# Keys and values by seven products ahead of the up projection, and up results masked and turned on chip

## The chip, the cores and the metric

One core of a Trainium2 chip runs the whole kernel in one launch. The metric is the device time of one execution in microseconds (us), the median of several runs. In rows of the profile, PE is TensorE's matmul, PEld its weight load, DVE VectorE, ACT ScalarE, POOL GpSimd, SP the SyncE queue that issues most DMAs.

## The reference

A post-norm decoder layer over x of 16 x 112 tokens of 1024 numbers (1792 tokens, 14 tiles of 128) with a context of 16 x 375 tokens (6000) of 1024:

```python
s = silu(x @ w_gate.T)                     # 1792 x 2752
s = s with the 1376 smallest |s| of each row set to 0
h = s * (x @ w_up.T)
x = layernorm(x + h @ w_down.T)
q, k, v = x @ Wq, ctx @ Wk, ctx @ Wv       # k, v: 256 wide, 8 heads of 32, each for 4 of 32 query heads
x = layernorm(x + softmax(q k.T / sqrt(32)) v @ Wo)
x = layernorm(x + x @ dequantized 4-bit weights, in bfloat16)
```

All products but the last are float32.

## The kernel before, in words

The work is one program for one core. Each engine's instructions are kept in the order in which they were written (`AsWritten`), so the order of the Python calls is the order of each engine's queue. Up to the down projection everything happens in `gates_up_keys`.

There a `stream` of work items is made: 24 plain gate chunks (`gate_chunk`, tiles 0 to 3, 464 or 456 columns), then 20 gate units and 28 up units (`up_unit`), then 16 x 5 items of keys and values (`kv_unit`). `emit` takes the next item, issues its matmuls into one of six PSUM banks (`ps_g`), and then issues the evacuation of the item before it (`behind`, `settle(1)`). Each item has a weight, about the columns of its eight-matmul product.

A gate or up unit takes two token tiles (a pair) and one of four column passes of each half of the 2752 columns (344 of 1376), and forms the four 128 x 344 results by seven products instead of eight (Strassen's method in Winograd's form; the order of the products is `ORDER`). A product is 4 f32 matmuls, 8 records in the trace. It needs sums of x tiles (`xs_d`, made once by `sums_of_x` on GpSimd) and sums of weight blocks (`sum_weights`, 16 instructions on GpSimd for each set of weights; a set serves 2 or 3 pairs of gates, or 7 pairs of up). The results are combined in the evacuations: in the gates by copies on ScalarE and adds on VectorE, two of which (L410, L417) read two SBUF tiles; in the up units those two run on GpSimd. Gate results go through silu to `s_d` in DRAM. Up results are multiplied with s (read back from `s_d`) on GpSimd (L393) and stored to `u_d`.

Beside the stream runs the search for the median of |s| of each row. `search(t)` handles one tile of 128 rows in 12 steps: the absolute values on ScalarE, seven counts (ScalarE counts 1824 columns at L556, VectorE 928 at L559), a selection (L622), the eight largest (L624), the mask (L638), and a flag over all rows (L641) on which VectorE branches: if a row was not settled, a slow search runs. Then the mask of 2752 bfloat16 goes to `m_d` by a DMA of the GpSimd queue (L647). Two searches alternate, and after each step `beside` emits `share` of the stream's weight. The share spreads the 14 searches over the stream up to its last 14 batches of keys and values:

```python
steps = len(DAMPS) + 6
ends = (B - 2) * (2 + NKP)
share = sum(w for w, _ in list(stream)[:-ends]) / (steps * TT)
```

`load_row(t)` first emits the stream until the gates of tile t are stored whole, and then loads the row tile from `s_d`. Rows of a pair become whole with the last pass of their weights.

Keys and values are computed per batch of 375 context tokens: two items of keys (256 outputs on the partitions, 375 columns, L452), three of values (tokens on the partitions, 256 columns, L460), each of 8 f32 matmuls. Beside them `next_turn` reads u and the mask back, multiplies them on GpSimd (L506), transposes the product on TensorE (L524, 308 transposes in all), copies it (L526) and stores it to `hT_d`, from which the down projection (`Down`, L827) loads its blocks. `load_down` loads down weights, `down.first_product` begins the down projection. Loads and most stores are issued on SP; `store_later` holds a store back by two items.

After that come the down projection's passes, queries, attention, the output projection and the 4-bit product; the change touches only how attention reads keys and values from `k_d` and `v_d`.

Of the kernel before, what the change touches and what calls it, by code (L numbers as in the profile page):

```python
# [22 lines left out]
P = 128  # L23
# [23 lines left out]
H_CHUNKS = [(h * FH + o, w) for h in range(2) for o, w in ((0, 512), (512, 512), (1024, 352))]  # L47
UPASS = 4
UW = FH // UPASS
# [85 lines left out]
def gates_up_keys(  # L135
    nc, tc, order, ident, xT, wg, wu, ctxT, wk, wv, s_d, m_d, u_d, xs_d, hT_d, k_d, v_d, down,
# [22 lines left out]
    search_ctx, io_ctx, w_ctx = (ExitStack() for _ in range(3))  # L159
# [5 lines left out]
    wpool = w_ctx.enter_context(tc.tile_pool(name="g_w", bufs=1, side="right"))  # L165

# [34 lines left out]
    def load_others():  # L201

        for tag, size, ts_ in (("lo0", 5120, (4, 5, 6, 7, 12)), ("lo1", 5632, (8, 9, 10, 11, 13))):
            o = room(lo, tag, f"xo_{tag}", size, len(ts_), KC, P)
            for i, t in enumerate(ts_):
                xts[t] = o[:, i]
                load_x(t)

    def sums_of_x(j):
# [14 lines left out]
        0: lambda: load_x(1), 4: lambda: load_pair(1), 6: load_others, 8: lambda: sums_of_x(2), 10: lambda: sums_of_x(3),  # L224
        11: lambda: sums_of_x(4), 12: lambda: sums_of_x(5), 13: lambda: sums_of_x(6),
        14: lambda: load_weights(0), 15: lambda: sums_of_x(0), 18: lambda: deque(sum_weights(0, 0), 0),
        20: lambda: sums_of_x(1), 21: lambda: load_first(0),
# [37 lines left out]
    sets = [(wg, p, js) for js in GATE_PAIRS for p in range(UPASS)]  # L265
    sets += [(wu, p, tuple(range(pairs))) for p in range(UPASS)]
    units = [(k, j) for k, (_, _, js) in enumerate(sets) for j in js]
    n_gate = sum(w is wg for w, _, js in sets for _ in js)
# [4 lines left out]
    def load_weights(k):  # L273

        w, p, _ = sets[k]
        if k % 2:
            u = room(upool[0], "w0", f"u0_{k}", 3 * KH * UW, 3, KH, UW)
            v = room(upool[0], "w1", f"u1_{k}", 4 * KH * UW, 4, KH, UW)
        else:
            u = room(lo, "lo0", f"u0_{k}", 5120, 3, KH, UW)  # L280
            v = room(lo, "lo1", f"u1_{k}", 5632, 4, KH, UW)
        for to, i, h in ((u[:, 0], 0, 0), (u[:, 2], 0, 1), (v[:, 0], 1, 0), (v[:, 1], 1, 1)):
            nc.sync.dma_start(to, w[:, ts(i, KH), ds(h * FH + p * UW, UW)])
        wts[k] = u, v
# [19 lines left out]
    def load_rest(i):  # L304

        j = units[i][1]
        a = rest[i] = room(upool[0], "l", f"xl_{i}", 3 * KH * P, 3, KH * P, bufs=2)
        nc.sync.dma_start(a[:, :2], xs_d[j].rearrange("p h k n -> p h (k n)")[:, 2:])
        nc.sync.dma_start(a[:, 2], xT[2 * j + 1][:, KH:].rearrange("p k n -> p (k n)"))

    def side_loads(i):
        if i + 1 < n_up:
            load_first(i + 1)
            load_rest(i + 1)
        if i == n_up - 4:
            load_keys()

    sums = deque()

    def side_weights(i, b):  # L320

        k, j = units[i]
        at, n = sets[k][2].index(j), len(sets[k][2])
        if at == b == 0:
            sums.append(sum_weights(k, 1))
        if b == 1 and at == 0 and k + 1 < len(sets):
            load_weights(k + 1)
        if b == 0 and at == n - 1 and k + 1 < len(sets):
            sums.append(sum_weights(k + 1, 0))
        for _ in range(1 if at else 2):  # L330
            while sums and next(sums[0], sums) is sums:
                sums.popleft()
# [4 lines left out]
    def load_s():  # L337
        if s_order:
            i, t, h = s_order.pop(0)
            k, j = units[i]  # L340
            s = room(io, "s", f"us_{i}_{t}_{h}", 512, UW, bufs=5)
            nc.sync.dma_start(s, s_d[2 * j + t][:, ds(h * FH + sets[k][1] * UW, UW)])
            s_ahead.append((i, t, h, s))

    def silu():

        while unsaid and unsaid[0][0] >= len(stream) + 2:
            _, i, t, h, a = unsaid.popleft()
            k, j = units[i]
            nc.scalar.activation(a, a, AF.Silu)  # L350
            last = sets[k][1] == UPASS - 1 and (t, h) == (1, 1)
            store_later(
                s_d[2 * j + t][:, ds(h * FH + sets[k][1] * UW, UW)], a,
                (2 * j, 2 * j + 1) if last else (),
            )

    def up_unit(i, what):

        k, j = units[i]
        p, gate = sets[k][1], i < n_gate  # L360
        adds = nc.vector if gate else nc.gpsimd
# [8 lines left out]
        if what == "A11 B11":  # L370
            if i == n_gate:
                for _ in range(4):
                    load_s()
            side_loads(i)
        m = ps_g.tile([P, 512], F32, tag="pg", name=f"pu_{i}_{what[:2]}_{b}")[:, :UW]
        for n in range(KH):
            nc.tensor.matmul(  # L377
                m, a[i][:, b, ts(n, P)], w[:, n, :], start=(n == 0), stop=(n == KH - 1)
            )
        side_weights(i, ORDER.index(what))  # L380

        def own(tag):
            st[tag] = room(upool[0], tag, f"{tag}_{i}", 384, UW, bufs=3 if tag == "u" else 2)
            return st[tag]

        def store(t, h, tag):
# [4 lines left out]
            *of, s = s_ahead.popleft()  # L391
            assert of == [i, t, h]
            nc.gpsimd.tensor_tensor(a, a, s, ALU.mult)  # L393
            store_later(u_d[2 * j + t][:, ds(h * FH + p * UW, UW)], a)
            load_s()

        def evacuate():
            silu()
            if what == "A11 B11":
                nc.scalar.copy(own("c11"), m)  # L400
            elif what == "S2 T2":
                nc.vector.tensor_add(own("u"), st["c11"], m)  # L402
            elif what == "A12 B21":
                nc.vector.tensor_add(st["c11"], st["c11"], m)
                store(0, 0, "c11")
            elif what == "S1 T1":
                nc.scalar.copy(own("m5"), m)
            elif what == "S4 B22":
                nc.vector.tensor_add(own("c12"), st["u"], m)
                adds.tensor_tensor(st["c12"], st["c12"], st["m5"], ALU.add)  # L410
                store(0, 1, "c12")
            elif what == "S3 T3":
                nc.vector.tensor_add(st["u"], st["u"], m)
            else:
                nc.vector.tensor_add(own("c21"), st["u"], m)
                store(1, 0, "c21")
                adds.tensor_tensor(st["u"], st["u"], st.pop("m5"), ALU.add)  # L417
                store(1, 1, "u")
# [3 lines left out]
    ctxs, kv = {}, {}  # L422

    def load_ctx(b):
        tag, size = ("w0", 3 * KH * UW) if b % 2 else ("ctx", KC * SK)
        ctxs[b] = room(upool[0], tag, f"ctx_{b}", size, KC, SK)
        nc.sync.dma_start(ctxs[b], ctxT[b])

    def load_keys():
        kv["k"] = upool[0].tile([P, KC, KVD], F32, tag="wk", name="wk_sb")  # L430
        nc.sync.dma_start(kv["k"], wk)
        load_ctx(0)

    def kv_unit(b, u):
        if b == u == 0:
            kv["v"] = room(upool[0], "w1", "wv_sb", 4 * KH * UW, KC, KVD)
            nc.sync.dma_start(kv["v"], wv)
            for tag, n in (("lo0", 10), ("lo1", 11)):
                to_load.extend(down.place(lo, tag, n, 1))
        next_turn()  # L440
        if u == 0 and b < B // 2:
            next_turn()
        if u == (1 if b else 0) and b + 1 < B:
            load_ctx(b + 1)
        if u in (1, 3):
            load_down()
        c = ctxs[b]
        pk = ps_g.tile([P, 512], F32, tag="pg", name=f"pk_{b}_{u}")
        if u < 2:
            n, w, to = P, SK, k_d[b, :, u, :]  # L450
            for kc in range(KC):
                nc.tensor.matmul(  # L452
                    pk[:, :SK], kv["k"][:, kc, ts(u, P)], c[:, kc, :],
                    start=(kc == 0), stop=(kc == KC - 1),
                )
        else:
            at = (u - 2) * P
            n, w, to = min(P, SK - at), KVD, v_d[b, ds(at, P), :]
            for kc in range(KC):
                nc.tensor.matmul(  # L460
                    pk[:n, :KVD], c[:, kc, ds(at, n)], kv["v"][:, kc, :],
                    start=(kc == 0), stop=(kc == KC - 1),
                )

        def evacuate():
            o = room(upool[0], "u", f"kv_{b}_{u}", 384, SK, bufs=3)
            if n < P:
                nc.gpsimd.memset(o[P - Q :, :w], 0.0)
            nc.scalar.copy(o[:n, :w], pk[:n, :w])
            store_later(to, o[:, :w])  # L470

        return evacuate
# [7 lines left out]

    to_turn = deque((t, c) for t in range(TT) for c in range(len(H_CHUNKS)))
    found, asked, ready = set(), deque(), deque()
    n_asked = 0

    def load_turn():

        nonlocal n_asked
# [1118 lines left out]
```

## Time and profile before

| | us |
|---|---|
| median of 3 runs | 2512.85 (2509.98 to 2514.65) |
| profiled execution, time | 2511.96 |
| profiled execution, span | 2510.2 |
| PE busy in the span | 2469.8 |
| stage: plain gates | to 157 |
| stage: gate units | 157 to 482 |
| stage: up units | 482 to 938 |
| stage: keys, values and turns | 938 to 1302 |
| first pass of down and after | from 1302 |

The stage bounds are where the first matmul of the next stage starts in the timeline, rounded. The granted TensorE clock is 0.992 of full speed over the span. The page is read as follows: its second part cuts the span into 40 slices of 62.8 us and gives the busy tenths of each engine in each; the groups give the mean time of one instruction and the idle time before it; the waits say who waited for whom. Durations of matmul records overlap in the groups (a 344-column record has a mean of 452 ns, but eight of them take 2.31 us in the chain), so the chain is the better place for the price of one. In a timeline row the columns are start, duration, engine, line, operation, tiles, count, and in brackets the idle time before it with what ended it.

### The profile page before, as it was taken

The numbers are of one execution on the slowest core, as the hardware profiler recorded it, in microseconds if no ns is written. First come the engines' busy times: TensorE is split into PE (matmuls) and PEld (weight loads), VectorE is DVE, ScalarE is ACT, GpSimd is POOL, SyncE is SP. The second block draws the span as 40 slices with busy tenths as digits, with TensorE's granted clock in tenths as the row PEclk, the third lists the DMA queues.
The fourth block names the chain that finished last, engine by engine and source line by source line (L and its number), as shares of the span: only waits on it lengthen the run. The fifth ranks groups of instructions, "written<-read, shape, count | busy, mean of one in ns | idle before, by whom it ended". The sixth has DMA issues, their size and how long they took to land.

```text
span 2510.2 us, 33282 instructions
## 1 busy us (share of the span) xinstructions
PE 2469.8 (98%) x10674; PEld 1555.1 (62%) x10674; DVE 1232.8 (49%) x2020; ACT 791.8 (32%) x1872; POOL 1139.6 (45%) x1145
## 2 busy tenths in 40 slices
PE   9999999999999999999999999999999999999998
PEld 4456666666666667777764444444666666767764
DVE  0257767655555552000000442157667877777764
ACT  0233333333323322222110000000455655555653
POOL 1755413336364633222200000023578788888874
PEclk9999999999999999999999999999999999999999
DMA  9567866877787759887764222266876778777774
GB/s 358 210 221 267 284 239 233 282 253 271 234 285 235 231 200 323 280 278 253 244 218 158 81 90 95 82 217 209 195 189 188 198 192 209 193 198 197 188 179 118
DMA packets 321749, 538.15 MB, mean 214 GB/s; under 512 B 41984, under 2 KB 238976, under 8 KB 317440
## 3 DMA queue, kind: packets, MB, share of 16 engines
q1 hardware_dynamic: 283136, 447.41, 56.3%
q0 software_dynamic: 23168, 61.66, 8.3%
q10 hardware_dynamic: 15232, 26.62, 3.4%
q8 instruction: 87, 1.43, 0.2%
q14 instruction: 126, 1.03, 0.1%
HBM read 331.37 MB, written 103.50 MB: 173 GB/s over the span
## 4 chain that ended last, share of the span: by engine, by line
PE 76%; DVE 2%; DMA 2%; ACT 2%; issue 1%; POOL 1%; SPq 1%; ACTq 0%; POOLq 0%; DVEq 0%
PE m L827 18%; PE pu_S L377 13%; PE pu_A L377 9%; PE pk L460 7%; PE bank L1218 7%; PE pk L452 6%; PE bank L1056 5%; PE sc L1126 4%; PE po L1181 3%; PE bank L1275 2%; PE pt L524 1%; ACT probs L1134 1%; DMA weights<-squares 1%; DVE nmax L1132 1%; DVE squares L1154 1%
## 5 line engine op out<-in xcount | busy, mean ns | idle before, releaser
L1143 POOL TENSOR_TENSOR probs<-probs,sums 128x1500 f32<-128x1500 f32 x128 | 344.2, 2691 | 122.6 <-DVE sums L1142 110.3
L1134 ACT ACTIVATE probs<-sc,nmax 128x375 f32<-128x375 f32 x512 | 286.9, 573 | 231.6 <-DVE nmax L1132 216.9
L1132 DVE TENSOR_REDUCE nmax<-sc 128x2 f32<-128x750 f32 x256 | 228.5, 932 | 136.6 <-PE sc L1126 136.6
L556 ACT ACTIVATE ja<-a,to 128x1824 int8<-128x1824 f32 x98 | 177.9, 1815 | 283.4 <-DVE to L616 268.6
L827 PE MATMUL m<-wd,h 128*128 128x512 f32 (+1 forms) x616 | 265.0, 592 | 0.0
L377 PE MATMUL pu_A<-u,xe 128*128 128x344 f32 x768 | 237.9, 453 | 1.9 <-DVE u L402 1.9
L377 PE MATMUL pu_S<-u,xe 128*128 128x344 f32 x768 | 237.8, 452 | 0.1
L1154 DVE STREAM_TRANSPOSE squares<-probs 128x1536 f32<-128x1536 f32 x128 | 224.1, 1751 | 17.5 <-DMA weights<-squares 10.6
L377 PE MATMUL pu_S<-u,xl 128*128 128x344 f32 x768 | 229.9, 452 | 0.0
L901 DVE TENSOR_TENSOR c<-u,m 128x512 f32<-128x512 f32 x7 | 4.8, 688 | 436.1 <-DMA h<-hT_d 354.9
L1056 PE MATMUL bank<-x1T,wq_sb 128*128 128x224 f32 x1008 | 210.6, 363 | 0.0
L1056 PEld LDWEIGHTS bank<-x1T,wq_sb 128*128 128x128 f32 x1008 | 188.3, 192 | 34.8 <-issue 31.2
L827 PEld LDWEIGHTS m<-wd,h 128*128 128x128 f32 (+1 forms) x616 | 116.8, 190 | 146.7 <-issue 145.4
L377 PEld LDWEIGHTS pu_A<-u,xe 128*128 128x128 f32 x768 | 145.8, 190 | 78.9 <-DVE u L402 3.0
L1218 PE MATMUL bank<-wo_sb,aT 128*128 128x256 f32 x832 | 194.2, 387 | 0.0
L377 PEld LDWEIGHTS pu_S<-u,xe 128*128 128x128 f32 x768 | 145.8, 190 | 76.6 <-issue 0.6
L377 PEld LDWEIGHTS pu_S<-u,xl 128*128 128x128 f32 x768 | 145.9, 190 | 76.2
L1218 PEld LDWEIGHTS bank<-wo_sb,aT 128*128 128x128 f32 x832 | 154.9, 191 | 46.1 <-issue 23.7
L1168 POOL DMA_DIRECT2D weights<-squares x320 | 178.6, 564 | 8.8 <-issue 4.1
L506 POOL TENSOR_TENSOR hs<-hs,hm 128x512 f32<-128x512 f32 (+1 forms) x84 | 90.0, 1078 | 199.6 <-DMA hm<-m_d 188.3
L460 PE MATMUL pk<-wv_sb,ctx 128*128 128x256 f32 (+1 forms) x768 | 173.3, 379 | 0.0
L452 PE MATMUL pk<-ctx,wk_sb 128*128 128x375 f32 x512 | 167.1, 478 | 0.0
(165 smaller groups left out, 3355.5 us busy)
## 6 DMA issues: line engine op xcount, KB each, us to landing
weights<-squares SPq DMA_DIRECT2D x704, 96.0 KB, 3.3
h<-hT_d SPq DMA_DIRECT2D x56, 640.0 KB, 4.5
weights<-squares POOLq DMA_DIRECT2D x320, 96.0 KB, 3.5
xe<-in_xT_dram SPq DMA_DIRECT2D x48, 512.0 KB, 5.1
xe<-xs_d SPq DMA_DIRECT2D x48, 512.0 KB, 5.9
xl<-xs_d SPq DMA_DIRECT2D x48, 512.0 KB, 5.0
ctx<-in_ctxT_dram SPq DMA_DIRECT2D x16, 1500.0 KB, 8.2
u<-in_wg_dram SPq DMA_DIRECT2D x32, 688.0 KB, 9.0
```

The costliest lines, as they stand in the source:

```text
L377: nc.tensor.matmul(m, a[i][:, b, ts(n, P)], w[:, n, :], start=(n == 0), stop=(n == KH - 1))
L452: nc.tensor.matmul(pk[:, :SK], kv["k"][:, kc, ts(u, P)], c[:, kc, :], start=(kc == 0), stop=(kc == KC - 1),)
L460: nc.tensor.matmul(pk[:n, :KVD], c[:, kc, ds(at, n)], kv["v"][:, kc, :], start=(kc == 0), stop=(kc == KC - 1),)
L556: nc.scalar.activation(ja, a[:, NV:], AF.Sign, bias=to, scale=-1.0, accum_out=st["sgn"])
L827: self.nc.tensor.matmul(bank, a[:r, k, :], b(k)[:r], start=(k == 0), stop=(k == HK - 1),)
L1056: nc.tensor.matmul(pq[:, :GT], self.wq_sb[:, kc, ts(mc, P)], self.x1T[g][:, kc, :], start=(kc == 0), stop=(kc == KC - 1),)
L1132: nc.vector.tensor_reduce(nmax[h], sc[h][:, :, :SK], AX.X, ALU.max, negate=True)
L1134: nc.scalar.activation(pr[:, i, :SK], sc[i // 2][:, i % 2, :SK], AF.Exp, bias=nmax[i // 2][:, i % 2 : i % 2 + 1], accum_out=sums[:, i : i ...
L1143: nc.gpsimd.tensor_tensor(pr, pr, sums.unsqueeze(2).to_broadcast([P, 4, SK]), ALU.mult)
L1154: nc.vector.transpose(sq[:, :, n % 2].rearrange("p k (i f) -> p k i f", f=Q), probs[:, n % 3].rearrange("p i (k f) -> p k i f", f=Q),)
L1168: queue.dma_start(wt[ts(m, Q), :, j], by_part[ts(j, Q), :, m])
L1218: nc.tensor.matmul(pp[:, :256], aT[:, h, r, :], wo_sb[:, h * REP + r, ts(i, 256)], start=(h == 0 and r == 0), stop=(h == 1 and r == REP - 1),)
```

## The change

The order of the stream becomes gates, keys and values, up.

- Keys and values are formed with the seven products too: six pairs of blocks of 500 context tokens (free columns), the contraction of 1024 in two halves, the 256 outputs in two halves. Both keys and values have outputs on the partitions now. The weight sums are made once (`sum_kv_weights`), the sums of context blocks on GpSimd (`sum_ctx`, 16 instructions of 128 x 500 for a pair). Values are then transposed on TensorE (`turn_values`) and copied on ScalarE. All the combining adds run on VectorE.
- The up passes are 384, 384, 384 and 224 columns wide. For each up result the mask is loaded with s; VectorE multiplies s with the mask (`mask_s`), GpSimd the result with that, TensorE transposes it three items later (`turn`), and it goes to `hT_d`. `u_d` and its traffic are gone. The two adds that ran on GpSimd in the up units run on VectorE.
- The searches get a fixed pace of 2400 units of stream weight per tile (`PACE`), so that the masks are there before the up units. The stream may be emitted beside them up to the last pair of keys and values.
- The SBUF pools change hands between stages (`gate_swap`, `kv_swap`, `up_swap`); the down weights are loaded during the up units. `k_d` and `v_d` are laid out over all 6000 context tokens.

The core of the diff:

```diff
+GATE_PASSES = [(0, 344), (344, 344), (688, 344), (1032, 344)]
+UP_PASSES = [(0, 384), (384, 384), (768, 384), (1152, 224)]
+KVN = 500
+KV_PAIRS = B * SK // KVN // 2
+PACE = 2400
...
     def load_s():
...
+            m = pools["w"].tile([P, UW], BF16, tag="um", name=f"um_{i}_{t}_{h}", bufs=5)[:, :n]
+            nc.sync.dma_start(s, s_d[2 * j + t][:, at])
+            nc.sync.dma_start(m, m_d[2 * j + t][:, at])
+    def mask_s():
+        if s_ahead:
+            *_, s, m = s_ahead[0]
+            nc.vector.tensor_mul(s, s, m)
...
+    def combine(st, what, m, own, done):
...
+        elif what == "S4 B22":
+            nc.vector.tensor_add(own("c12"), st["u"], m)
+            nc.vector.tensor_add(st["c12"], st["c12"], st["m5"])
+            done(0, 1, "c12")
...
+            nc.vector.tensor_add(own("c21"), st["u"], m)
+            done(1, 0, "c21")
+            nc.vector.tensor_add(st["u"], st["u"], st.pop("m5"))
+            done(1, 1, "u")
...
             nc.gpsimd.tensor_tensor(a, a, s, ALU.mult)
-            store_later(u_d[2 * j + t][:, ds(h * FH + p * UW, UW)], a)
+            to_turn.append((len(stream), i, t, h, a))
+            mask_s()
             load_s()
...
+    def sum_ctx(i, names):
...
+            for n in range(KH):
+                nc.gpsimd.tensor_tensor(
+                    out[:, n], ctxs[i, y][:, n], ctxs[i, z][:, n], ALU.subtract
+                )
+                yield
+    FIRST_SUMS = (("T1", "B12", "B11"), ("T2", "B22", "T1"))
...
+    def beside_kv(i, b, x):
+        if x == "k":
+            if b == 0:
+                if i == 0:
+                    sums.append(sum_ctx(i, FIRST_SUMS))
+                    sum_some(8)
+                sums.append(sum_ctx(i, (("T3", "B22", "B12"),)))
+            if b == 2:
+                sums.append(sum_ctx(i, (("T4", "B21", "T2"),)))
...
+                if b == 5:
+                    sums.append(sum_ctx(i + 1, FIRST_SUMS))
...
+        sum_some(2)
+    def kv_unit(i, b, x):
...
+        turns_of_values()
...
+        m = products(
+            f"p{x}_{i}_{what[:2]}", what, lambda n: kv[x][:, o, n, :], ctxs[i, name]
+        )
+        beside_kv(i, b, x)
...
+    def turns_of_values(behind_=2):
+        while values_to_turn and values_to_turn[0][0] >= len(stream) + behind_:
+            _, at, c, a = values_to_turn.popleft()
+            turn_values(at, c, a)
...
+    def kv_swap():
+        settle(0)
+        silu(-NT)
+        issue(-NT)
+        w_ctx.close()
+        pools["kv"] = w_ctx.enter_context(tc.tile_pool(name="u_kv", bufs=1, side="right"))
+        load_ctx(0, 1, 1)
+        load_ctx(0, 1, 0)
...
+    for i in range(KV_PAIRS):
+        for b in range(len(ORDER)):
+            for x in "kv":
+                stream.append((KVN / 2, lambda i=i, b=b, x=x: kv_unit(i, b, x)))
+    stream.append((0, up_swap))
+    for i in range(n_gate, n_up):
+        for what in ORDER:
+            stream.append((sets[units[i][0]][2] / 2, lambda i=i, what=what: up_unit(i, what)))
...
-    ends = (B - 2) * (2 + NKP)
-    share = sum(w for w, _ in list(stream)[:-ends]) / (steps * TT)
+    ends = (n_up - n_gate) * len(ORDER) + 1 + 2 * len(ORDER)
+    share = PACE / steps
```

## The prediction

> **What bounds the kernel now.** I read the page first, then TensorE's waits, the chain, the windows by stage, and the timelines of VectorE and GpSimd in the gate stage. The page:
>
> ```profile
> PE 2469.8 (98%) x10674; PEld 1555.1 (62%) x10674; DVE 1232.8 (49%) x2020; ACT 791.8 (32%) x1872; POOL 1139.6 (45%) x1145
> ...
> DVE  0257767655555552000000442157667877777764
> ...
> POOL 1755413336364633222200000023578788888874
> ```
>
> TensorE (PE) works 2469.8 of 2510.2 us. The DVE row shows its reserve: 5 to 7 tenths busy in the gate and up products (slices 2 to 14), none in the keys and values (slices 15 to 20). TensorE's own waits confirm the bound: before attention they are a few us.
>
> ```profile
> PE pt L524 <- POOL hs L506: 2.1, 1, 2.1
> PE pu_A L377 <- DVE u L402: 1.9, 2, 1.3
> ```
>
> The chain gives the price of one matmul record without the overlap that the group rows hold (an f32 matmul is two records):
>
> ```profile
> 394.60 6.94 PE pu_S L377 x24
> ...
> 1286.35 5.06 PE pk L452 x16
> 1291.74 10.36 PE pk L460 x48
> 1302.10 443.94 PE m L827 x1034
> ```
>
> So 0.289 us at 344 columns, 0.316 at 375, 0.216 at 256, 0.429 at 512. The windows give the engines by stage (up to 482 gates, to 938 up, to 1302 keys and values; columns: PE, PEld, DVE, ACT, POOL, clock, DMA):
>
> ```profile
> 157.00:482.00 325.00, 323.02 (x1115) 211.30 (x1114) 223.92 (x397) 127.29 (x201) 129.08 (x139) 1.00 0.75 261
> 482.00:938.00 456.00, 456.00 (x1577) 299.36 (x1576) 238.10 (x514) 136.27 (x172) 213.69 (x221) 1.00 0.74 250
> ```
>
> In the gates VectorE is 69% busy at one search in 65 us (the flags' reductions, L641, lie at 302.46 and 367.46). The change halves that distance, so I looked at what stops VectorE there. VectorE, then GpSimd:
>
> ```profile
> 302.46 0.27 DVE L641 TENSOR_REDUCE flag<-row 1x1 int32<-1x128 f32 x1
> 307.94 0.51 DVE L415 TENSOR_TENSOR c<-u,pu_A 128x344 f32<-128x344 f32 x1 [5.22 <-issue]
> 308.49 10.71 DVE L417 TENSOR_TENSOR u<-u,m 128x344 f32<-128x344 f32 x1
> ```
> ```profile
> 304.29 0.56 POOL L647 DMA_DIRECT2D m_d<-m  x1 [18.26 <-DVEq L121]
> 304.88 3.52 POOL L294 TENSOR_TENSOR u<-u 128x344 f32<-128x344 f32 x4
> 308.36 6.99 POOL L294 TENSOR_TENSOR u<-u,u 128x344 f32<-128x344 f32 x8
> 315.31 3.52 POOL L294 TENSOR_TENSOR u<-u 128x344 f32<-128x344 f32 x4
> ```
>
> The branch after the flag keeps VectorE 5.2 us. The mask's store sits in GpSimd's queue behind that branch, and the weight sums pile up behind it; once released they run back to back, and VectorE's add of two SBUF tiles (0.52 us elsewhere) does not finish before the last of them, 10.2 us late. After each of the first five mask stores one two-input VectorE instruction waited so: 6.0, 10.1, 10.2, 9.8 and 4.6 us, mean 8.2. TensorE felt little of it: out of service from 302.7 to 321.2 but for one add, VectorE cost TensorE 1.3 us. Six PSUM banks cover some 13 us, once.
>
> **The change part by part.**
>
> *Keys and values by seven products.* Before: 16 batches of 32 records at 0.316 and 48 at 0.216, 16 x 20.5 = 328 us. After: 6 pairs x 2 x 7 products x 8 records = 672 records of 500 columns, 0.429 x 500/512 = 0.419 us, 282 us. Minus 46 us, on the path.
>
> *Values turned on TensorE.* 24 results x 4 transposes = 96. Four lie between 951.18 and 951.62 in TensorE's timeline, 0.11 us each: plus 11 us. The 308 transposes of h keep their number.
>
> *Up products 384 wide and 224 once.* 1176 records at 0.289 x 384/344 = 0.323 and 392 at 0.196 (nearest row: the queries' 224 columns, 32 in 6.27 us) make 457 us, against 1568 x 0.289 = 453: plus 3 us.
>
> *The way of u through DRAM.* It takes away 84+28 stores and 84 loads, 39 MB, and its 4 us of waiting at the start of the keys (the two waits above, roughly). Its DMA time lies beside TensorE, which works all 456 us of the up window at DMA 0.74: the transfers themselves are worth nothing. The mask's product goes to VectorE, idle in the new up stage: 112 x 0.6 us more, plus 56 adds, is 100 us in 457. GpSimd keeps 112 products of 0.95 us. The turns come three products (8 us) behind, over a sum and a product of 2 us: hidden. VectorE waits at the swap some 5 us (loads land in 4.5), which the banks cover. I take 0 for these, 0 to 5 for the range.
>
> So TensorE's own work falls by 46 + 4 - 11 - 3 = 36 us.
>
> *The searches, one per 2400 units of stream.* A unit is 16.2 us / 1204 = 13.45 ns: 32.3 us per search. Before: (5040 + 20 x 1204 + 28 x 1204 + 3326)/14 = 4726 units, 64 us. Work of one search on VectorE, from starts in the timeline: six counts 2.10 each, first count 1.4, b 3.3, best 4.0, m 1.65, flag and branch 5.4: 28.4 us. It fits alone, but not with the adds of the products, 3.5 us per gate unit.
>
> Where do the dense parts lie? The loop asks for row 4 after 36 steps of 200 units (7200; 5040 are plain chunks, so near unit 1.8) and must first emit gates up to unit 7.7, where rows 4 to 7 are whole. From there 48 steps, 4 searches, run over 9600 units = 8 gate units to 15.7; then row 8 forces emission to 18.6. The last 7 searches take 16,800 units, 1700 in the gates and 15,100 in the keys, 4.3 pairs of six.
>
> Gates 7.7 to 15.7: TensorE 8 x 16.2 = 130 us. VectorE 4 x 28.4 + 8 x 3.5 = 142, plus the wait after each mask store: row 8.2 us, four times, 33. Less 13 us of cover: plus 32 us. Bounds for that wait: below, 0.4 us (the two-input L616 at 213.46, beside running sums, waited 0.36); above, 10 us. So 0 to 39.
>
> *Swap to the keys.* T2 needs a block of ctx loaded into the space of the gate weights, behind the last unit's stores on SP: about 2.5 us to the last silu, 5 landing, four GpSimd sums of 1.28 (row of 128x512, L220): 12.6 us, against two products of 3.35. Plus 6; 0 if the load comes early, 13 if nothing is covered.
>
> *Keys and values, 4.3 pairs beside 6.3 searches.* TensorE 4.3 x (47 + 2) = 211 us. VectorE 6.3 x 28.4 + 4.3 x 14 adds of 0.6 = 215, plus a wait after each mask store: GpSimd now has 16 ctx sums a pair, about 11 per mask, of 1.28 us. I keep 8.2 us as measured (0.4 to 14): 52. The cover is smaller: the turn of a value stands in TensorE's queue two products, 6.7 us, behind the product whose sum it reads, and all matmuls queue behind it. Plus 215 + 52 - 211 - 7 = 49 us; 0 to 85.
>
> Sum: -36 + 32 + 6 + 49 = +51 us on the profiled execution's 2512.0 us (span 2510.2 and 1.8 around it; the median is 2512.9, so no correction): 2563 us.
>
> [...]
>
> **The rivals.**
>
> *VectorE keeps up: faster.* If the pile behind a mask store lets VectorE in after one sum, as at 213.46, the stalls are 12 - 13, so none, in the gates, none in the keys, and 6 at the swap: 2512 - 36 + 6 = 2482. For it: sums that came as their data landed did let VectorE in. Against: none of the first five mask stores went so. It decides at a wait of 3.3 us per store: with a wait of x the stalls are 4x - 1 and 6.3x - 3, and they eat the 30 us left at 3.3.
>
> *Worse: lag feeds on itself.* A late VectorE delays the mask store, so GpSimd's sums (T2, weights) come late too and TensorE waits for them directly; the flag waits for a row DMA in an SP queue held by late stores. With the upper ends: -36 + 39 + 13 + 85 = +101, 2613. For it: GpSimd already waited up to 51 us at that store. Against: forced emission leaves VectorE pauses to catch up.
>
> *It doesn't do what it says.* Searches still running when up begins would move, not vanish; the count above ends them 1.7 pairs ahead, so I give it little, within the cases above.
>
> **How the numbers follow.** VectorE-bound dense parts 0.56; faster rival 0.24; nearly even, a wait near 3.3 us, 0.05; worse 0.15. Some 0.2% (5 us) is what a measurement of this kernel can tell from no change. Range 2484 to 2613: the low end reaches to the faster rival, the high one to the upper bounds. Faster 0.24, same 0.05, slower 0.71.
>
> **What would show it.** Right: TensorE's waits on DVE, on POOL's sums and before the value turns at 30 us or more in gates and keys together; VectorE 8 or 9 tenths busy there and slack in up; two-input adds of 5 to 14 us behind mask stores; TensorE records of keys and values at 0.42 us. Wrong: TensorE without waits up to the up stage (then 2482), or waits placed in the up stage or at its end.

## The result and the profile after

The change makes the kernel slower: 2579.98 us median (2578.94 to 2582.74) beside 2513.6 us for the kernel before, a ratio of 1.0268, 95% interval 1.0251 to 1.0286. The profiled execution has a span of 2577.1 us, 66.9 more than before. The page after, first part and four rows of the second:

```profile
PE 2454.0 (95%) x10148; PEld 1458.7 (57%) x10162; DVE 1376.0 (53%) x2274; ACT 792.6 (31%) x1892; POOL 1119.5 (43%) x1094
...
PE   9989987989889999999999999999989999999997
...
DVE  0374476568773233333331342238677777777764
...
POOL 1754312352434224242320000023487888888874
PEclk9999998999999999999999999999989999999999
```

TensorE has less work (2454.0 against 2469.8 us) in a longer span. The holes in its row (slices of 64.4 us, counted from 0) lie in slices 2, 5, 6, 8, 10 and 11, that is between 129 and 773 us, in the gates and the keys and values. The seven largest of TensorE's thirteen kinds of wait from 150 to 900 us (line, whom it waited for: us in total, times, longest):

```profile
PE pu_A L402 <- ACT m L417: 18.0, 3, 9.3
PE pv L644 <- DVE v_ops L425: 14.6, 4, 6.8
PE pu_S L402 <- DVE c L425: 11.6, 1, 11.6
PE pk_S L402 <- POOL T L562: 8.9, 1, 8.9
PE pv L644 <- DVE to L738: 4.7, 2, 2.4
PE pt L491 <- DMA u<-in_wu_dram: 4.2, 1, 4.2
PE pv L644 <- DVE off L743: 4.1, 2, 2.3
```

Before, this list held two entries of 2 us. Four of these seven releasers are VectorE, and the largest is a ScalarE copy; why that one is VectorE's doing too is seen below. The stages in windows (gates, keys and values, up; columns as in the prediction):

```profile
158.00:530.00 372.00, 335.96 (x1121) 216.68 (x1120) 217.44 (x434) 132.47 (x206) 121.55 (x137) 0.94 0.68 232
530.00:869.00 339.00, 304.64 (x764) 141.28 (x763) 220.00 (x420) 123.08 (x172) 144.08 (x119) 0.95 0.47 153
869.00:1365.00 496.00, 488.90 (x1876) 327.33 (x1875) 167.21 (x307) 71.66 (x192) 158.93 (x158) 1.00 0.72 232
```

The gates' 1121 records take 372 us (before: 1115 in 325), and the granted clock, 1.00 there before, is 0.94. The lines do not show a full VectorE: 58% busy in the gates, 65% in the keys. One stop in the gates shows what they hide. First all engines, then TensorE's own timeline, then two windows (the seventh column is the clock):

```profile
348.01 0.48 ACT L393 ACTIVATE u<-u 128x344 f32<-128x344 f32 x1
...
348.18 0.27 DVE L775 TENSOR_REDUCE flag<-row 1x1 int32<-1x128 f32 x1
348.38 0.49 DVE L414 TENSOR_TENSOR c<-c,pu_A 128x344 f32<-128x344 f32 x1
...
350.00 0.56 POOL L781 DMA_DIRECT2D m_d<-m  x1 [34.61 <-DVEq L125]
350.58 0.92 POOL L305 TENSOR_TENSOR u<-u 128x344 f32<-128x344 f32 x1
351.45 6.98 POOL L305 TENSOR_TENSOR u<-u,u 128x344 f32<-128x344 f32 x8
...
355.72 0.21 DVE L743 TENSOR_SCALAR off<-sgn,nlt 128x1 f32<-128x1 f32 x1 [6.85 <-issue]
...
356.52 5.39 DVE L750 SCALAR_TENSOR_TENSOR to<-off,to 128x1 f32<-128x1 f32 x1
...
362.01 1.81 ACT L690 ACTIVATE ja<-a,to 128x1824 int8<-128x1824 f32 x1 [13.52 <-DVE to L750]
...
363.82 0.42 ACT L417 COPY m<-pu_S 128x344 f32<-128x344 f32 x1
```
```profile
353.28 2.59 PE L402 MATMUL pu_S<-u,xe 128*128 128x344 f32 x8
364.30 4.96 PE L402 MATMUL pu_A<-u,xe 128*128 128x344 f32 x8 [8.43 <-ACT m L417]
```
```profile
364.00:370.00 6.00, 5.70 (x10) 3.54 (x11) 5.61 (x16) 5.24 (x7) 0.00 (x0) 0.50 0.28 67
374.00:384.00 10.00, 10.00 (x36) 6.55 (x35) 9.60 (x17) 3.48 (x7) 0.00 (x0) 1.00 0.80 303
```

The branch after the flag keeps VectorE 6.85 us. The mask's store, queued behind that branch, lets GpSimd's weight sums go at once, and the two-input L750 (0.16 us elsewhere) waits 5.2 us beside them. ScalarE's next instruction is the count that needs L750's result; it stands 13.5 us, and behind it in ScalarE's order stands the copy L417 that frees a bank. So TensorE waits 8.43 us "for ScalarE". Then it runs on at half the clock: eight records take 4.96 us, elsewhere 2.48.

### The profile page after: what moved, and what is told of

Its sections match the earlier page's. It is cut to its first block, busy times and chain, and to the rows that moved or that the text cites. A ratio compares the mean times of both kernels' runs of the same rounds, so it can differ in the third digit from the quotient of the medians.

```text
span 2577.1 us, 32248 instructions
## 1 busy us (share of the span) xinstructions
PE 2454.0 (95%) x10148; PEld 1458.7 (57%) x10162; DVE 1376.0 (53%) x2274; ACT 792.6 (31%) x1892; POOL 1119.5 (43%) x1094
## 4 chain that ended last, share of the span: by engine, by line
PE 54%; DMA 4%; DVE 4%; issue 2%; ACT 2%; POOL 1%; SPq 0%; ACTq 0%; DVEq 0%; POOLq 0%
PE m L981 14%; PE pu_S L402 9%; PE pu_A L402 7%; PE bank L1373 6%; PE bank L1210 5%; PE sc L1281 3%; PE po L1336 3%; PE bank L1430 1%; ACT probs L1289 1%; PE pt L491 1%; DVE nmax L1287 1%; PE pk_S L402 1%; PE pv_S L402 1%; DVE ln_st L81 1%; DMA weights<-squares 1%
## 5 line engine op out<-in xcount | busy, mean ns | idle before, releaser
L402 PE MATMUL pu_A<-u,xe 128*128 128x384 f32 (+2 forms) x768 | 243.2, 460 | 18.0 <-ACT m L417 18.0
L402 PE MATMUL pu_S<-u,xl 128*128 128x384 f32 (+2 forms) x768 | 232.6, 456 | 12.1 <-DVE c L425 11.6
L402 PE MATMUL pu_S<-u,xe 128*128 128x384 f32 (+2 forms) x768 | 240.2, 456 | 0.0
L463 POOL TENSOR_TENSOR c<-c,us 128x384 f32<-128x384 f32 (+1 forms) x84 | 89.1, 1061 | 342.7 <-DVE c L420 147.3
L402 PEld LDWEIGHTS pu_A<-u,xe 128*128 128x128 f32 x768 | 148.4, 194 | 98.4 <-ACT m L417 19.7
L402 PEld LDWEIGHTS pu_S<-u,xl 128*128 128x128 f32 x768 | 146.7, 191 | 90.0 <-DVE c L425 12.1
L402 PEld LDWEIGHTS pu_S<-u,xe 128*128 128x128 f32 x768 | 142.6, 192 | 67.0 <-issue 2.1
L240 PE MATMUL pg<-wg_sb,xp 128*128 128x456 f32 (+1 forms) x384 | 148.4, 549 | 3.9 <-DMA wg_sb<-in_wg_dram 3.9
L1281 PE MATMUL sc<-kT,qT 32*128 32x375 f32 x1024 | 138.0, 531 | 14.6 <-ACT probs L1289 9.9
L1111 POOL TENSOR_TENSOR y<-y,c 128x512 f32<-128x512 f32 x7 | 9.6, 1376 | 324.4 <-DMA q<-in_qw_dram 324.2
```

The lines of the kernel that those rows point to most:

```text
L240: nc.tensor.matmul(pg[:, :w], xts[t][:, kc, :], wg_sb[:, kc, ds(off, w)], start=(kc == 0), stop=(kc == KC - 1),)
L402: nc.tensor.matmul(m, a(n), k[:, n, :], start=(n == 0), stop=(n == KH - 1))
L1281: nc.tensor.matmul(sc[i // 2][:, i % 2, :SK], q[ts(i, HD), c * REP + r, ds(b % GB * (GT - P), P)], kt[ts(i, HD), :], start=True, stop=True,)
```

## The experiments

**The theory:** VectorE is out of service too long and too often once the searches are packed into gates and keys. The rival: the new stage itself costs the time (the swap, the value turns, the context sums), or the up units with their turns. Stages are measured from the first matmul of one to that of the next in the timeline of the profiled execution, whose time can lie off the median (e5: 2577.6, e8: 2520.7, e9: 2534.5); "idle" is TensorE's waiting in it, waits over 0.3 us; all in us. The gate units of before, counted by their 1120 records, end at 484.7, not at 482:

| kernel | median | ratio to before (95%) | gates: length, idle | keys, values: length, idle | down starts |
|---|---|---|---|---|---|
| before | 2513.6 | | 326.6, 2 | 363.6, 2 (with the turns of h) | 1301.9 |
| after | 2580.0 | 1.0268 (1.0251, 1.0286) | 372.3, 35.8 | 338.4, 33.9 | 1365.5 |
| e1_before_dense | 2597.6 | 1.0323 (1.0303, 1.0342) | with up 863.3, 59.1 (before 780.3, 2) | 365.7, 2.5 | 1385.8 |
| e12_before_dense_no_branch | 2548.8 | 1.0131 (1.0114, 1.0148) | with up 813.1, 25.6 | 363.6, 2.0 | 1333.4 |
| e4_light_search | 2505.7 | 0.9963 (0.9949, 0.9977) | 332.5, 6.4 | 304.5, 8.5 | 1289.8 |
| e2_no_branch | 2533.0 | 1.0067 (1.0044, 1.0089) | 353.7, 20.8 | 312.0, 15.3 | 1315.6 |
| e11_flag_no_branch | 2527.6 | 1.0046 (1.0032, 1.0060) | 348.4, 18.9 | 313.0, 14.0 | 1312.5 |
| e3_paced | 2537.2 | 1.0092 (1.0076, 1.0109) | 327.1, 1.3 | 341.2, 37.5 | 1324.0 |
| e10_paced_no_branch | 2510.5 | 0.9989 (0.9978, 0.9999) | 323.9, 0 | 323.2, 23.6 | 1297.5 |
| e5_mask_store_later | 2589.1 | 1.0293 (1.0276, 1.0311) | 371.2, 32.3 | 345.4, 41.6 | 1368.8 |
| e6_turns_4_behind | 2603.2 | 1.0351 (1.0334, 1.0368) | 372.3, 35.6 | 354.2, 45.7 | 1387.4 |
| e7_combined | 2536.9 | 1.0069 (1.0046, 1.0093) | 337.0, 9.0 | 325.5, 26.7 | 1327.4 |
| e8_combined_b22 | 2531.2 | 1.0062 (1.0045, 1.0079) | 328.7, 3.2 | 322.3, 22.9 | 1307.7 |
| e9_paced_b22_share | 2527.6 | 1.0045 (1.0028, 1.0061) | 329.0, 4.0 | 333.4, 34.0 | 1315.9 |

**e1: the old kernel with the new density of searches.** The second edit emits the gates and up units whole before the searches' buffers close.

```diff
-    share = sum(w for w, _ in list(stream)[:-ends]) / (steps * TT)
+    share = 2400 / steps
...
+    while len(stream) >= B * (2 + NKP):
+        emit()
     search_ctx.close()
```

> The kernel before, with one search per 2400 units of stream instead of 4726; order of stages, keys, values and up as before. Theory A (VectorE is overloaded where the searches run at the dense pace, and TensorE waits for its evacuations): the gate stage grows by about what it grew in the changed kernel, 48 us (372 us against 325), with TensorE waits on VectorE and ScalarE of 25 to 45 us, and the up stage by 0 to 20, since its products need only five VectorE adds; 2550 to 2580 us. Theory B (the waits come from the new stage itself: value turns close behind, context sums, swap of pools): within 10 us of 2513.

The density alone, without any other part of the change, makes the old kernel 83 us slower; the whole change costs 66. The gate units of e1 alone take 376.0 us with 36.3 idle, as in the changed kernel (372.3, 35.8). Its up units lose 34 us (22.9 idle), more than was expected, and take the total past the expected range. The first and the third of TensorE's largest waits are those of the change, under the old line numbers; those on L402 lie in the up units:

```profile
PE pu_A L377 <- ACT m L407: 17.5, 3, 9.3
PE pu_A L377 <- DVE u L402: 12.4, 5, 3.1
PE pu_S L377 <- DVE c L415: 10.0, 2, 8.6
```

**e4: the change with almost no counting.** Each of the seven counts reads 64 columns on each engine (ScalarE 1824 before, VectorE 928), and flag and branch are gone. Its masks are therefore not the right ones; the instructions that use them are the same.

```diff
-            ja, a[:, NV:], AF.Sign, bias=to, scale=-1.0, accum_out=st["sgn"]
+            ja[:, :64], a[:, NV : NV + 64], AF.Sign, bias=to, scale=-1.0, accum_out=st["sgn"]
...
-            jv, a[:, :NV], to, NA / 2 - TOPK - MID, ALU.is_lt, ALU.add, accum_out=st["nlt"]
+            jv[:, :64], a[:, :64], to, NA / 2 - TOPK - MID, ALU.is_lt, ALU.add, accum_out=st["nlt"]
```

> The changed kernel with counts over 64 columns on each engine instead of 928 and 1824, and without flag and branch: the masks are then wrong, all else runs. A search costs VectorE some 15 us instead of 28 and more. Theory A: what is left is TensorE's own work, the swap to the keys (about 10 us) and a few us in up; 2487 to 2505 us, which also tests the 36 us that the products save. Theory B: the 25 us before the value turns and in the swap stay, and the gates' waits too; 2550 to 2580.

With the searches' load gone, the rest of the change is a small gain: down starts 12 us earlier than before, the total is 0.37% shorter. The rival falls: keys and values take 304.5 us, up 494.9 (after: 496.9). But it is not the 36 us of lighter TensorE work either; 20 us of waits are left (6.4 gates, 8.5 keys, 5.1 up).

**e2, e11, e12: the branch.** e11 takes `value_load`, `Switch` and its slow arm out of the new kernel and keeps row DMA and flag; e12 does the same in e1; e2 drops row DMA and flag too. In all three, as in e4, a row that the quick search did not settle would have no second search.

```diff
-        which = nc.vector.value_load(flag, min_val=0, max_val=1)
-        for arm in order.arms(tc.Switch({mybir.EngineType.DVE: which}, 2)):
-            if arm:
-                halves = b.bitcast(BF16)
-                by_bits(a, st, halves[:, :FF], halves[:, FF:].bitcast(U16), m)
```

> The changed kernel without the flag, the branch on it and the slow search in its arm (part of the computation left out: a row that the fast search did not settle stays as it is). Theory A, branch and pile-up as its main parts: VectorE loses 5 to 9 us less per search and the mask store no longer holds GpSimd's sums; TensorE's waits fall from 36 to under 10 us in the gates and from 34 to 10 to 20 in the keys, the slow records after them go too; 2505 to 2535 us. Theory A, pure load of counts as its main part: 2545 to 2565. Theory B: 2570 to 2580.

> The changed kernel with row DMA and flag, but without the branch on it. If the 47 us of the run without both lie in the branch itself (5 to 9 us of an idle VectorE each): 2530 to 2540. If a good part was the wait of VectorE for the row's DMA, or of GpSimd's mask store behind it: 2550 to 2575.

> The old kernel with the 14 searches dense (one per 2400 units), without the branch on the flag. If the branch is a cost of dense searches only, and the same one in the old order: the 83 us that the dense searches cost there fall to 30 to 50, 2545 to 2565. If the branch costs only in the new order: 2585 to 2600.

The branch is the largest single cost: 52 us of the new kernel (2580.0 to 2527.6), 49 of the dense old one (2597.6 to 2548.8); with the paces of e3 it is 27 (2537.2 to 2510.5, e10). e2 is no faster than e11, so the row's DMA and the flag cost nothing measurable; it is the branch. It does not work through the waits of the two-input instructions: these are longer in e11's gates (34 us above their usual duration in waits over 1 us, after: 21). VectorE, GpSimd and TensorE in e11, from three timelines:

```profile
325.38 12.13 DVE L427 TENSOR_TENSOR u<-u,m 128x344 f32<-128x344 f32 x1
```
```profile
325.22 0.56 POOL L776 DMA_DIRECT2D m_d<-m  x1 [22.71 <-DVE m L772]
325.81 0.93 POOL L305 TENSOR_TENSOR u<-u 128x344 f32<-128x344 f32 x1
326.68 6.99 POOL L305 TENSOR_TENSOR u<-u,u 128x344 f32<-128x344 f32 x8
333.63 3.50 POOL L305 TENSOR_TENSOR u<-u 128x344 f32<-128x344 f32 x4
```
```profile
340.77 4.96 PE L402 MATMUL pu_A<-u,xl 128*128 128x344 f32 x8 [5.90 <-ACT c L410]
```

Without a branch the store waits for the mask itself, the pile behind it is the same, and an add waits 11.6 us for all of it: a stop of 12.1 us costs TensorE 5.9, where branch and block together cost it 8.4.

**e3, e10: the pace.** More of the stream is emitted per search, most of all beside the first tiles, so the searches lie more evenly (after has no flag between 180 and 308 us, e3 two).

```diff
-    share = PACE / steps
+    share = [p / steps for p in (4400,) * 4 + (3200,) * 4 + (2700,) * 6]
...
-                beside()
+                beside(t)
```

> The changed kernel with its searches spread as far as rows and masks allow: 4400 units for tiles 0 to 3, 3200 for 4 to 7, 2700 for 8 to 13, instead of 2400 for all. Theory A: waits in the gates under 10 us (VectorE 28.4 + 9.3 of adds per 43 us), in the keys 15 to 30 (36 us of pace against 34 of work); 2510 to 2540 us. Theory B: 2560 to 2580.

> The changed kernel with the three paces and without row DMA, flag, branch and slow arm (a row that the search didn't settle would keep a wrong mask). If dense VectorE work and the branch are all that the change loses: gates without idle (327), keys and values near 305 to 315 with the swap, 2496 to 2510. If there is a third cause (transfers, queues, the swap): 2515 to 2530.

The paces alone take 43 us off: the gates' idle time falls from 35.8 to 1.3 while that of the keys hardly moves (33.9 to 37.5). That is not because the gates hold less of the searches. From 300 to 480 us both kernels have four flags with a branch, at 308, 348, 394 and 440 in after and 301, 351, 396 and 437 in e3, and VectorE (third column) is busier in e3. First after, then e3:

```profile
300.00:480.00 180.00, 156.16 (x508) 99.28 (x507) 124.20 (x261) 83.27 (x119) 47.33 (x55) 0.92 0.64 219
300.00:480.00 180.00, 178.10 (x612) 115.67 (x611) 131.98 (x278) 85.00 (x126) 55.33 (x60) 1.00 0.71 241
```

What differs is what stands behind the four branches: in e3 it is each time an add that evacuates a product; in after it is a search step at three of the four, and at two of these L750 then waits 5.2 and 3.7 us beside GpSimd's sums, with ScalarE's copies behind it (e3 has one such wait, 8.2 us on an add). So in this stretch the gain does not come from a lighter load. That it comes from this order of the instructions is read from the traces; no run changes the one without the other.

With the branch gone as well (e10, the edits of e2 and e3) the loss is gone: 0.9989. The two causes overlap: 43 and 47 us (e2) singly, 69.5 together. Of what is left in e10's keys, 23.6 us, 4.8 are the swap and 16.8 two stops behind the pile, now of context sums. The first of them:

```profile
518.89 0.57 POOL L772 DMA_DIRECT2D m_d<-m  x1 [14.04 <-DVE off L743]
519.48 4.83 POOL L562 TENSOR_TENSOR T<-B,B 128x500 f32<-128x500 f32 x4
524.27 4.89 POOL L562 TENSOR_TENSOR T<-B,T 128x500 f32<-128x500 f32 x4
529.13 4.81 POOL L562 TENSOR_TENSOR T<-B,B 128x500 f32<-128x500 f32 x4
```
```profile
519.30 14.66 DVE L750 SCALAR_TENSOR_TENSOR to<-off,to 128x1 f32<-128x1 f32 x1
```
```profile
537.98 1.12 PE L644 MATMUL pv<-ident,v_ops 128*128 128x128 f32 x4 [8.93 <-DVE v_ops L420]
```

**e5: the mask's store five stream items later,** on the same queue, so that GpSimd does not stand behind the branch.

```diff
-        nc.gpsimd.dma_start(m_d[t], m)
+        masks.append((len(stream), t, m))
...
+    def store_masks(behind_=5):
+        while masks and masks[0][0] >= len(stream) + behind_:
+            _, t, m = masks.popleft()
+            nc.gpsimd.dma_start(m_d[t], m)
```

> The changed kernel with the mask's store issued on the GpSimd queue five stream items later, so that GpSimd's sums no longer pile up behind the branch. If the pile-up is a main part of VectorE's overload: the two-input waits of over 1 us (16 us in the gates from tile 4 on and at 189, 15 us in the keys) go, and with them 15 to 30 us; 2550 to 2565. If the branch and the counts alone saturate VectorE: 2570 to 2582.

A miss. GpSimd's waits at the store fell from 243.5 us in 12 to 115.6 in 7 (from 150 to 870 us), but the gates kept 32 of 36 us of idle time, and the keys gained 8. The two-input waits that it should have ended moved: 16 us in the gates and 22 in the keys (after: 21 and 15), in waits over 1 us. So this run does not say what they cost.

**e6: the value turns four products behind instead of two.**

```diff
-    def turns_of_values(behind_=2):
+    def turns_of_values(behind_=4):
```

> The changed kernel with the turns of the values four items behind their sums instead of two (13.4 us of cover instead of 6.7). If the short cover makes TensorE wait in the keys: the 25 us before the value turns fall under 10, with the slow records after them; 2550 to 2562. If VectorE is simply behind there: TensorE waits for PSUM banks instead; 2572 to 2582.

A miss, and 23 us worse. More distance gave no cover: TensorE's wait before the turns has a longest of 11.4 us (after: 6.8), and the up stage has a wait of 12.1 us. That the value results have one buffer each, so that VectorE waits for their turns, is my reading of the code; no run separates it.

**e7, e8, e9: combinations.** e7 is e3, e5 and e6 together. e8 adds the up turns four behind and the first B22 loaded ahead of the swap. e9 is e3 with that B22 and with VectorE counting 448 columns instead of 928.

```diff
+        if (i, name) == (0, "B22"):
+            a = room(io, "e", f"{name}_{i}", 4 * KH * P, KH, KVN, bufs=2)
...
-NV = 928
+NV = 448
```

> Paced searches (4400, 3200, 2700), mask store five items later, value turns four items behind. By the overload theory the gates run at 325 to 328 us, the keys at 305 to 320 (swap 11, few other waits): 2505 to 2522. If the three only shift the same wait: not under 2530.

> As the run before it, with the first B22 block of the context loaded ahead into a free buffer of the gates (so that T2 of the first pair doesn't wait for a load behind the last stores), and the turns of up results four items behind instead of three. Swap wait 11 us to under 4, the waits before the turns in up (5 to 9 us) to under 3: 10 to 15 us under that run, 2494 to 2510, at or under the kernel before. If these waits are covered by others: no difference.

> The changed kernel with the three paces (4400, 3200, 2700), the first B22 of the context loaded before the swap, and of each row 448 columns counted by VectorE instead of 928 (ScalarE counts the other 2304). VectorE's count falls by about 0.5 us, 88 counts in gates and keys 44 us, ScalarE gains some 0.4 us each, with ScalarE under half busy. If the loss that is left with the paces (2537) is VectorE's work in the keys and values: their idle time falls from 37 us to 15 to 25, 2512 to 2522. If it is the branch and the order of the queues at the swap, not work: 2528 to 2537. If ScalarE's longer counts come to hold up its copies: slower than 2537.

e7 is level with e3. e8 and e9 come to 1.0062 and 1.0045: the best that keeps every part of the computation is still slower than the old kernel. In e9 VectorE counts half as much (and ScalarE more), and the keys still idle 34.0 us (e3: 37.5). Without the swap that is 19.6 against 26.0: lighter counting may have helped there, but most of the waiting is not set by the sum of VectorE's work. The early B22 did not shorten the swap, 14.4 us in e9 (e3: 11.5). Its rows, VectorE, GpSimd, TensorE:

```profile
486.19 0.27 DVE L778 TENSOR_REDUCE flag<-row 1x1 int32<-1x128 f32 x1
493.80 0.51 DVE L420 TENSOR_TENSOR c<-u,pu_S 128x344 f32<-128x344 f32 x1 [7.33 <-issue]
```
```profile
502.21 4.83 POOL L565 TENSOR_TENSOR T<-B,B 128x500 f32<-128x500 f32 x4 [13.29 <-ACT ja L693]
```
```profile
508.29 4.53 PE L403 MATMUL pk_S<-T,k_ops 128*128 128x500 f32 x5 [14.45 <-POOL T L565]
```

A branch fell on the last gate results, and the sums began 2.4 us after the last silu (ended 499.8). In after and in e4 they began 2.5 and 2.4 us after it too: which fits that the tiles of the sums take the space of the gate stage and wait for its last result. What came late was that result, not the loaded block.

Not tried: the mask's store on another queue than GpSimd's, and one flag and branch for several tiles.

## Why the prediction was right, and what its sum hid

The verdict holds, and the mechanism in the main: slower, because TensorE waits for VectorE in the packed part of gates and keys; 2563 was forecast, 2580 measured, inside the range. But VectorE does not have more work there than time, as the terms for gates and keys have it (142 us against 130): TensorE waits at single stops. By the forecast's steps:

*TensorE's own work, minus 36:* right in the main. It counts 4 us of waiting at the start of the keys as saved, of which 1.9 lay in the gates (two waits on L402, ending at 322 and 387 us). The keys' products take 3.35 us for eight records, as forecast:

```profile
799.50 3.35 PE pk_S L402 x8
802.86 3.35 PE pv_S L402 x8
```

Against 36 stand, up to the start of down, 76.8 us of idle time (35.8, 33.9 and 7.1) and 24 us of slow records (below): minus 36 + 101 = plus 65, measured 63.6. Another 3.3 us lie after it; their cause is open.

*Gates, plus 32:* measured plus 46 (372.3 against 326.6). Three terms were mis-sized. The two-input wait was put at 8.2 us after each mask store; in after it was 7.3, 5.2 and 3.7 in the gates and 6.1, 1.0, 4.6 and 3.0 in the keys, with none at the other stores: 31 us over 14 stores, 2.2 each. Flag and branch were put at 5.4, from flags near the one shown; over 13 flags of before the branch alone averages 6.85, and over the 14 of after the same (4.9 to 9.2). And the cover of 13 us failed. Before, the stop that began with the flag at 302.46 let TensorE run on to 320.5, 17.8 us: what stood behind the branch was an add that frees a bank (L415), and ScalarE's copy was ahead of its count. After, TensorE stood 7.0 us after VectorE stopped (348.87 to 355.87): behind the branch stood a search step, hit by the sums, and ScalarE's copy behind the count that needs it. A step was missing altogether: stops ahead of unit 7.7 were taken as free, and the one at 180 us (branch 7.9, then 7.3 beside the sums) cost 11.6 us.

*Swap, plus 6:* 8.9. The forecast had the last silu 2.5 us after the first key product and a loaded block behind it; the silu came 6.8 us after, and T1's four sums (4.8 us) had to come ahead of T2's first (1.2): 6.8 + 2.5 + 4.8 + 1.2 - 6.7 = 8.6.

*Keys and values, plus 49:* 33.9 us of idle time, the swap's 8.9 in it, and 11.5 of slow records: 36.5 without the swap. The waits (52) were too large, the slow clock was not in it.

*Up and the way of u, 0:* 7.1 us idle, 4.2 of it a wait for up weights at the start, which the range of 0 to 5 named for another reason.

So that the total came within 17 us is in part luck: the gates came out 14 us above their term, the up stage 7 and the swap 3, the keys 12 below theirs. The blocks of the two-input instructions, 85 in the sum, were 31 on VectorE in after. No run takes them alone away; without the branch they do stop TensorE, for 16 of the 18.9 us of idle time in e11's gates (behind two blocks of 11.5). What the sum had too small or not at all was what the branches cost in this order (52, e11) and the slow records (24). By the signs that were named: TensorE's waits of 30 us or more, measured 69.7; records of 0.42 us, right. VectorE at 8 or 9 tenths was wrong: 58 and 65% busy, and 70 and 79% with the branches' pauses (44 and 46 us), which count as idle though VectorE is out of service in them. Two-input adds of 5 to 14 us did not come: each of the seven blocks of after was on the one-column search step L750, three of them over 5 us.

*The length of a block:* blocks did last longer than one GpSimd instruction: 14.5 us over twelve context sums (e10), 11.6 over thirteen weight sums (e11). Others ended sooner: in after 3.0 us over three context sums (at 766.91) and 1.0 beside one (at 611.13). How long one lasts stays open.

*The rival "VectorE keeps up", 2482,* would have needed the searches free; e4, with hardly any counting and no branch, gives 2505.7 with 20 us of waits left, so 2482 was too low in any case. What short blocks alone would have given, no run shows.

## What to carry to other kernels

Take a data-dependent branch's pause times the number of branches as a first bound of its cost (here 14 x 6.85 = 96 us, worth 52, and 27 with the paces), and look at what stands behind it on the other engines: here a copy that frees a bank, behind a count that needs the stopped engine's result, made three engines wait for one (ScalarE 13.5 and TensorE 8.43 us behind VectorE's stop at the flag at 348). Cover measured in one stop need not hold in the next (17.8 us before, 7.0 after): by these traces it went with the instruction that stood behind the stop, and the denser packing had changed that. Where work is packed closer, first pack it in the old order and measure that alone.

## What the runs showed of the hardware

*The instruction queue moves packets in the branch's pause.* In the pause of the flag at 348 us it moved two; the DMA view of that window has

```profile
q14 instruction: 2, 0.02, 0.7%
```

Fourteen other pauses, nine of after and five of before, hold two to four packets and 0.02 or 0.03 MB each; three windows behind flags of e11, which has no branch, hold none. In all 14 pauses of after VectorE goes on 2.1 to 2.9 us after the last of these packets started, whether the pause is 4.9 or 9.2 us long. That VectorE waits for these packets is my reading of the times; no run separates it. The pause itself takes 4.9 to 9.2 us in after, up to 11.2 before (at the flag at 686.61).

*In after TensorE's clock fell behind some waits of about 2 us, and not behind others.* Eight gate records took 4.96 us after a wait of 8.43 (clock 0.50 from 364 to 370) and 4.83 after one of 11.57; eight key records 6.12 after 8.86, and 4.90 after only 2.30, against 3.52. But none was slow after waits of 2.26 and 2.36 us (ending at 698.53 and 739.86). In the trace of after the clock changes, between 1.00 and 0.50, only at times a whole number of 3.41 us apart (189.17, 202.82, 359.83, 370.07 and so on). The wait of 2.30 us lay inside one such step, and the next step ran at half the clock; so it went with one of 2.04 us (ending at 714.61). Those of 2.26 and 2.36 us were divided between two steps. The step with the wait of 2.30 us, the one behind it, and the stretch behind the wait of 2.36 us:

```profile
581.70:585.11 3.41, 1.11 (x4) 0.30 (x3) 3.17 (x10) 3.41 (x3) 0.00 (x0) 1.00 0.79 218
585.11:588.53 3.42, 3.42 (x8) 1.93 (x8) 3.38 (x6) 2.58 (x4) 0.00 (x0) 0.50 0.94 363
739.86:746.00 6.14, 6.14 (x18) 3.14 (x19) 5.81 (x11) 4.89 (x9) 6.14 (x4) 1.00 0.00 0
```

Summed over gates and keys (324 and 84 x 3.35 + 11 = 293 us of own work; e10's gates, without a wait, take 323.9), that is 12.5 + 11.5 = 24 us beyond 69.7 us of waiting, and in e1 863.3 - 59.1 - 778.4 = 26 beyond 59.1: by these sums a microsecond waited cost about 1.34 in after and 1.44 in e1, an estimate.
